# A transformer block on one core: one accumulator bank and four banks for maxima in attention, a written order and other splitting in the first projections, and the value bias added at the normalisation

## The chip, the core and the metric

The kernel runs on one core of a Trainium2 chip. A core has five engines that work side by side, each with its own queue of instructions in order: TensorE (PE, matrix products; its weight loads are listed apart as PEld), VectorE (DVE), ScalarE (ACT), GpSimd (POOL) and SyncE (SP, which here only issues DMAs). Matrix products end in PSUM, which has eight banks of 128 partitions by 512 numbers of 32 bits. POOL does not touch PSUM in this kernel; ACT and DVE empty it. The metric is the time of one execution in microseconds (us); lower is better.

## The reference

A block with layer norms after each part: attention whose four projections each have a low-rank addition, then a mixture of experts. Input is `x` of 2 x 1024 tokens with 512 numbers.

```python
def lora_linear(x, W, b, Bm, Am):
    out = jnp.einsum('bld,od->blo', x, W) + b
    upd = jnp.einsum('blr,or->blo', jnp.einsum('bld,rd->blr', x, Bm), Am)
    return out + SCALING * upd                      # rank 16, SCALING 0.5
q, k, v = (_split(lora_linear(x, ...)) for q, k, v)  # 16 heads of 32
scores = jnp.einsum('bhqd,bhkd->bhqk', q, k) * SCALE
attn = jax.nn.softmax(scores, axis=-1)
out = jnp.einsum('bhqk,bhkd->bhqd', attn, v)
x = _layernorm(x + lora_linear(out, Wo, bo, Bo, Ao))
x = _layernorm(x + _moe(x, ...))   # 8 experts, capacity 256, hidden 704, and one shared expert
```

The rows of `attn` add up to one, so a bias that is added to every value vector comes out of attention as the same bias, added to the output of the head.

## The kernel before

Products of full accuracy are made from three products of numbers cut to a shorter format: a number is split into a high part (a cast by ACT) and a low part (number minus high part, by DVE or POOL), and high x high, low x high and high x low are added up in PSUM.

The work comes in three stages.

*First projections* (0 to about 158 us of the span). The low-rank factors are folded into the weights: `split_lora` splits the two factors, `fold_w` multiplies them, `split_w` adds the product to the weight and splits it. `load_lora`, `load_w` and `load_xk` issue the DMAs from SP. The first block of x is projected to q with the loop over the contraction outermost (`proj_all`), so that it can begin when a quarter of the weights is there. `store_qk` adds the bias, splits the result and sends it to DRAM; `proj_v` adds the value bias `bv_bc` (the bias spread over all partitions by a DMA) and sends v to DRAM. In the last of the four x blocks, the first 12 steps of maxima (below) are mixed in.

*Attention* (about 158 to 604 us). There are 16 units `u` (2 batches x 4 groups of 4 heads x 2 blocks of 512 queries), each of 8 steps `t` of 128 keys. A step has four heads `h`. The softmax needs each query's maximum first: `s1_step` makes a tile of scores with queries on the partitions (L203) and DVE reduces it (L211); 32 such tiles a unit run 12 steps ahead (`LEAD`). `finish_max` transposes the maxima (`mp`) and puts them into the query operand as two more rows, so that the second score product (`st_step`, L641) comes out with the maximum subtracted, keys on the partitions. ACT turns it into exponentials `pt` (L650). Every second step `av_step` multiplies the exponentials of the two steps before by v into the unit's accumulator `avs[u]` in PSUM (L660). For the row sums, `adds` adds the exponentials of a unit's steps up: by DMAs that accumulate ("dd", issued by POOL, L678), by POOL ("pp", L681), or in the last units by DVE ("vv", L681). `finish` sums over the partitions on PE (`sm`, L694), `invert` takes the reciprocal by way of DRAM, and `normalize` makes the output in three parts: 0, accumulator times reciprocal (L733); 1, its high part `at_h` (ACT L738, DVE L736 in two units); 2, its low part `at_l` (L740). `oproj` projects a batch's output, adds the residual (`load_res`, `add_res`) and takes the norm's statistics.

The order of all engines in attention is written out. In each step there are four slots, one behind each head's score product. `S_AT[k][q]` gives for step k of a unit and slot q how many maxima tiles come before and after the other work of that slot. `FIN`, `REC` and `NRM` place `finish`, `invert` and the parts of `normalize`, as (units later, step, slot); `ADDS` places the additions, `RES_AT` and `RES_ADDS` the residuals. The key `None` holds for all units that are not named.

PSUM in the first two stages: three banks `one` (second scores, maxima transposes, row sums, projections), two banks `avp` (accumulators), three banks `s1p` (maxima tiles). `ptp` holds `PTB` buffers of exponentials in SBUF.

*Experts* (from about 604 us): the shared expert, the routing, and eight experts; the last expert's rows are normalised by `norm_root` (POOL) and `norm_rows_act` (ACT) and stored by POOL's indirect DMAs.

`tc.manual_schedule(engines=...)` keeps the named engines in the order of the program; the others are ordered by the framework's planner. In the first stage PE is always in program order (`MAN1`), and ACT, DVE and POOL (`MAN0`) only up to the end of the first `split_k` loop.

Of the kernel before, what the change touches and what calls it, by code (L numbers as in the profile page):

```python
# [9 lines left out]
F32 = mybir.dt.float32  # L10
# [22 lines left out]
LEAD = 12  # L33
LATE, OP_ONE = (0,), 1
NS = NU * 8
WARM, WCOL = 4, 256
OPER = 4
PTB = 14
OHB = 3
# [18 lines left out]
FIN = {None: (1, 4, 1), NU - 3: (1, 3, 1), NU - 2: (1, 2, 3)}  # L58
REC = {None: (1, 6, 3), NU - 3: (1, 5, 3)}
NRM = {  # L60
    None: ((2, 1, 0), (2, 1, 2), (2, 1, 2)),
    NU - 3: ((2, 0, 1), (2, 0, 1), (2, 0, 1)),
    NU - 2: ((1, 4, 1), (1, 4, 1), (1, 4, 1)),
# [3 lines left out]
S_AT = (  # L67
# [4 lines left out]
)  # L72
# [40 lines left out]
def kernel(  # L113
    ctx, tc, xT, x, wT, bqk, bvo, lora, wg, w13, w2, s13, s2, out
):
# [19 lines left out]
    pool.memset(expo, -0.5)  # L135
    bqk_sb = const.tile([P, 8], F32, name="bqk_sb")
    bo_bc = const.tile([P, D], F32, name="bo_bc")
# [96 lines left out]
    with ExitStack() as ph1, tc.manual_schedule(engines=MAN1):  # L234
# [15 lines left out]
        wl = [wp.tile([P, KC, D], F32R, name=f"wl{i}") for i in range(3)] + [wo_l]  # L250
        bv_bc = wp.tile([P, D], F32, name="bv_bc")

        def load_lora(i):
            raws = []
            for j in range(2):
                raws.append(next(lraw_s)[0:LR])
                sp.dma_start(out=raws[j], in_=lora[i, j])
            return raws
# [12 lines left out]
        def prep_w(i, raws, ba=None):  # L271
            ba = ba or split_lora(i, raws)
            for k, lp in enumerate([fold_w(i, ba, k) for k in range(KC)]):
                split_w(i, k, raws, lp)

        def split_lora(i, raws):
            ba = []
            for j, lo in ((0, 64), (1, 32)):
                t_ = sg.tile([LR, D], F32R, name=f"lora{i}{j}", tag=f"lora{j}", bufs=1)
                act.copy(t_, raws[j])  # L280
                rows = slice(lo, lo + R)
                dve.tensor_tensor(t_[rows], raws[j][rows], f(t_[rows]), ALU.subtract)
                ba.append(t_)
            return ba

        def fold_w(i, ba, k):
            if k == KC - 1:
                lp = avp.tile([P, 512], F32, name=f"lp{i}{k}", tag="av")
            else:
                lp = s1p.tile([P, 512], F32, name=f"lp{i}{k}", tag="s1")  # L290
            pe.matmul(lp, ba[0][:, k * P : k * P + P], ba[1], start=True, stop=True)
            return lp
# [47 lines left out]
        def store_qk(tb, w, g, o):  # L340
            b, c0 = tb // 2, (tb % 2) * 512
            bias = bqk_sb[:, w * 4 + g : w * 4 + g + 1]
            oh = sg.tile([P, 512], F32R, name=f"oh{tb}{w}{g}", tag="oh", bufs=OHB)
            ol = sg.tile([P, 512], F32R, name=f"ol{tb}{w}{g}", tag="ol", bufs=OHB)
            act.activation(oh, o, AF.Identity, bias=bias)  # L345
            dve.scalar_tensor_tensor(ol, o, bias, f(oh), ALU.add, ALU.subtract)
            sp.dma_start(out=qk_d[w, b, g, 0][:, c0 : c0 + 512], in_=f(oh))
            sp.dma_start(out=qk_d[w, b, g, 1][:, c0 : c0 + 512], in_=f(ol))

        def proj_v(tb, xs, t4):  # L350
            o = bank1(f"v{tb}{t4}")
            n = 0
            for k in range(KC):
                hi, lo = (z[:, t4 * P : t4 * P + P] for z in xs[k])
                for lhs, rhs in ((hi, wh[2]), (lo, wh[2]), (hi, wl[2])):
                    pe.matmul(o, lhs, rhs[:, k, :], start=n == 0, stop=n == 11)
                    n += 1
                    if n % 6 == 0:
# [29 lines left out]
        for k in range(KC):  # L388
            load_wk(1, k, r1)
        sp.dma_start(out=bqk_sb, in_=bqk)  # L390

        with tc.manual_schedule(engines=MAN0):
            dve.memset(bo_bc, 0.0)
            warm("hot", WARM)
            ba = split_lora(0, r0)
            lps = [fold_w(0, ba, k) for k in range(KC)]
            warm("warm", 1)
            os_ = [bank1(f"o00{g}") for g in range(NG)]
            xs = []

            def split_k(k):
                split_w(0, k, r0, lps[k])
                xs.append(split_xk(0, k, x0[k]))


            def proj_all(k):
                hi, lo = xs[k]
                for i, (w_, x_) in enumerate(((wh, hi), (wl, hi), (wh, lo))):
                    for g in range(NG):
                        a = w_[0][:, k, g * P : g * P + P]  # L410
                        pe.matmul(os_[g], a, x_, start=k + i == 0, stop=False)

            pool.memset(f(Ks[0][96:98, :, :]), -1.0)
            for k in range(KC):
                split_k(k)
                if k == 1:
                    ba1 = split_lora(1, r1)
            pool.memset(f(Ks[1][96:98, :, :]), -1.0)
        for k in range(KC):
# [5 lines left out]
            if k == KC - 3:  # L425
                prep_w(1, r1, ba1)
        for tb in range(4):
            if tb == 0:
                for g in range(NG):
                    store_qk(0, 0, g, os_[g])  # L430
                    if g == 1:
                        sp.dma_start(out=bv_bc, in_=bvo[0:1, :].partition_broadcast(P))
                        r2 = load_w(2)
                for g in range(NG):
                    proj_qk(tb, xs, 1, g)
                    if g == 1:
                        prep_w(2, r2)
            else:
# [7 lines left out]
            for t4 in range(4):  # L446
                proj_v(tb, xs, t4)
                if t4 == 1 and tb < 3:
                    xn = split_x(tb + 1, xr)
            if tb == 0:  # L450
                sp.dma_start(out=bo_bc, in_=bvo[1:2, :].partition_broadcast(P))
                prep_w(3, load_w(3))
# [169 lines left out]
    with ph2, tc.manual_schedule(engines={mybir.EngineType.PE}):  # L622
# [31 lines left out]
        def av_step(t):  # L654
# [4 lines left out]
            for h in range(4):  # L659
# [7 lines left out]
                )  # L667

        def adds(t):
            u, kc = t // 8, t % 8  # L670
# [57 lines left out]
        def normalize(u, parts=(0, 1, 2)):  # L728
            g, qb = u // 2, u % 2
            cs = slice(qb * 512, qb * 512 + 512)  # L730
            hi, lo = at_h[:, g % NG, cs], at_l[:, g % NG, cs]
            if 0 in parts:
                dve.tensor_tensor(avs[u], avs[u], fin[u], ALU.mult)  # L733
            if 1 in parts:
                if u in NRM_DVE:
                    dve.tensor_copy(hi, avs[u])  # L736
                else:
                    act.copy(hi, avs[u])  # L738
            if 2 in parts:
                dve.tensor_tensor(lo, avs[u], f(hi), ALU.subtract)  # L740

# [59 lines left out]
        for t in range(NS):  # L801
# [433 lines left out]
    with tc.manual_schedule(engines=MAN4):  # L1235
# [123 lines left out]
```

## Time and profile before

| | |
|---|---|
| time, three runs | 1046.94, 1047.83, 1050.71 us (median 1047.83) |
| profiled execution, its own time | 1045.05 us |
| its span, first to last instruction | 1043.3 us |
| mean granted TensorE clock | 0.991 |
| first projections | 0 to 158 us |
| attention | 158 to 604 us |
| experts, to the end | 604 to 1043 us |

A row of groups gives line, engine, operation, output and inputs by the program's names, shapes and count, then busy time in us, mean duration of one in ns, and the idle time of the engine in front of it with what ended it. A row of the timeline gives start, duration, engine, line, operation, names and shapes, how many in a row, and in brackets the idle time before. A matmul's end is modelled and overlaps the next one's start, so that a PE that is busy all the time can still be held up; the distance of starts tells.

### The profile page before, as it was taken

What the parts mean: (1) busy time and instruction counts of PE and PEld (TensorE: products, weight loads), DVE (VectorE), ACT (ScalarE), POOL (GpSimd) and SP (SyncE); (2) the same over time, 40 slices, a digit from 0 to 9 for tenths busy, and PEclk for the clock granted to TensorE, in tenths of its full rate; (3) what the DMA queues carried; (4) which work ended last, traced back from release to release, by engine and by line L of the source; (5) the groups of instructions that cost most, each with busy time, mean ns of one, the idle gap of its engine ahead of it and who ended that gap; (6) DMA issues with size and microseconds to landing.
All of it is one profiled execution on the core that took longest, in us unless ns stands there. A gap on an engine that the chain in (4) does not pass through costs nothing. (4 is left out here: it accounts for less than half of the span.)

```text
span 1043.3 us, 15652 instructions
## 1 busy us (share of the span) xinstructions
PE 1016.6 (97%) x5606; PEld 722.7 (69%) x5606; DVE 676.1 (65%) x1156; ACT 520.4 (50%) x985; POOL 536.1 (51%) x404
## 2 busy tenths in 40 slices
PE   8999999999999999999999799999999999999994
PEld 6888784544444456654444279988788899999994
DVE  7732788788878877788877774222253467777752
ACT  5422206666666656576666645222132356555662
POOL 4000006889888977879895155000006056666674
PEclk9999999999999999999999899999999999999998
DMA  9876875686868783587974532000109667777721
GB/s 291 283 230 210 248 211 118 125 186 137 190 134 187 160 181 83 115 168 155 197 163 92 132 104 70 22 21 1 40 1 293 212 198 237 255 244 258 224 82 60
DMA packets 87374, 164.75 MB, mean 158 GB/s; under 512 B 15944, under 2 KB 24648, under 8 KB 87296
## 3 DMA queue, kind: packets, MB, share of 16 engines
q1 hardware_dynamic: 74240, 117.59, 38.8%
q0 software_dynamic: 13056, 46.16, 19.9%
q8 instruction: 44, 0.72, 0.3%
q14 instruction: 34, 0.28, 0.1%
HBM read 96.10 MB, written 33.80 MB: 125 GB/s over the span
## 5 line engine op out<-in xcount | busy, mean ns | idle before, releaser
L211 DVE TENSOR_REDUCE mt<-s 128x1 f32<-128x512 f32 x512 | 318.4, 681 | 75.2 <-PE s L203 75.1
L650 ACT ACTIVATE pt<-st 128x512 f32<-128x512 f32 x512 | 266.3, 618 | 147.5 <-PE st L641 145.6
L681 POOL TENSOR_TENSOR pt<-pt,pt 128x1024 f32<-128x1024 f32 x112 | 264.2, 2387 | 33.4 <-DMA pt<-pt 18.1
L203 PE MATMUL s<-ks,qs 96*128 96x512 f32 x512 | 196.1, 416 | 1.5 <-DVE mt L211 1.0
L641 PE MATMUL st<-qs,ks 98*128 98x512 f32 x512 | 189.3, 417 | 2.7 <-ACT pt L650 1.7
L678 POOL DMA_DIRECT2D pt<-pt x64 | 56.3, 1008 | 195.2 <-PE s L203 164.7
L641 PEld LDWEIGHTS st<-qs,ks 98*128 98x128 f32 x512 | 94.8, 189 | 72.5 <-ACT pt L650 26.8
L203 PEld LDWEIGHTS s<-ks,qs 96*128 96x128 f32 x512 | 94.2, 188 | 72.7 <-DVE mt L211 44.5
L924 PE MATMUL h<-xthe,w13s 128*128 128x256 f32 x704 | 129.9, 283 | 0.0
L924 PEld LDWEIGHTS h<-xthe,w13s 128*128 128x128 f32 x704 | 110.6, 191 | 0.4
L924 PE MATMUL h<-xtle,w13s 128*128 128x256 f32 x352 | 100.2, 285 | 0.0
L912 POOL TENSOR_TENSOR w2s<-w2r,w2s 128x512 fp32r<-128x512 f32 x42 | 65.8, 1588 | 64.9 <-ACT w2s L911 56.3
L1114 POOL DMA_INDIRECT xd_d<-x1a,slot_i x8 | 7.9, 985 | 139.3 <-DVE slot_i L1111 137.2
L660 PE MATMUL av<-pt,vt 128*32 128x512 f32 x512 | 64.0, 613 | 4.3 <-DVE at_l L740 4.3
L924 PEld LDWEIGHTS h<-xtle,w13s 128*128 128x128 f32 x352 | 67.3, 191 | 0.7
L660 PE MATMUL av<-pt,x1b 128*32 128x512 f32 x512 | 61.6, 598 | 0.0
L1010 PE MATMUL y<-w2s,hs 128*128 128x512 f32 x260 | 60.9, 390 | 0.0
L1010 PEld LDWEIGHTS y<-w2s,hs 128*128 128x128 f32 x260 | 48.3, 188 | 10.2 <-DVE hs L992 0.5
L589 DVE TENSOR_TENSOR w13s<-x1a,w13s 128x1024 fp32r<-128x1024 f32 x32 | 47.0, 1468 | 6.5 <-ACT w13s L583 6.5
L345 ACT ACTIVATE oh<-o,bqk_sb 128x512 fp32r<-128x512 f32 x32 | 21.9, 689 | 57.7 <-PE o L330 52.8
L583 ACT CAST w13s<-x1a 128x1024 fp32r<-128x1024 f32 x32 | 33.4, 1044 | 25.6 <-DMA x1a<-in_w_dram 19.4
L330 PE MATMUL o<-xh,wh 128*128 128x512 f32 x116 | 45.3, 391 | 0.0
(567 smaller groups left out, 1699.4 us busy)
## 6 DMA issues: line engine op xcount, KB each, us to landing
pt<-pt POOLq DMA_DIRECT2D x64, 512.0 KB, 7.9
x1a<-in_w_dram SPq DMA_DIRECT2D x32, 512.0 KB, 6.5
w2r<-in_w_dram SPq DMA_DIRECT2D x42, 256.0 KB, 3.2
ks<-qkd SPq DMA_DIRECT2D x36, 256.0 KB, 3.9
qkd<-oh SPq DMA_DIRECT2D x32, 256.0 KB, 2.9
qkd<-ol SPq DMA_DIRECT2D x32, 256.0 KB, 2.5
qs<-qkd SPq DMA_DIRECT2D x30, 256.0 KB, 5.1
qs<-qkd SPq DMA_DIRECT2D x36, 128.0 KB, 6.2
```

The lines of the kernel that those rows point to most:

```text
L203: pe.matmul(s1, Qs[u % 3][0:96, h, qt * P : qt * P + P], Ks[g % 2][0:96, h, kh * 512 : kh * 512 + 512], start=True, stop=True,)
L211: dve.tensor_reduce(mts[u][:, c, kh : kh + 1], s1, AX.X, ALU.max)
L330: pe.matmul(o, lhs, rhs, start=k + i == 0, stop=k + i == KC + 1)
L589: (pool if e < 0 else dve).tensor_tensor(lo, raw, f(hi), ALU.subtract)
L641: pe.matmul(sb, Ks[g % 2][:, h, kc * P : kc * P + P], Qs[u % 3][:, h, :], start=True, stop=True,)
L650: act.activation(pts[t, h // 2][:, h % 2, :], sb, AF.Exp, scale=SCALE)
L660: pe.matmul(avs[u][32 * h : 32 * h + 32, :], vts[g][:, kc, 32 * h : 32 * h + 32], pts[t, h // 2][:, h % 2, :], start=kc == 0, stop=kc == 7 ...
L678: pool.dma_start(out=pts[to, pr], in_=pts[i, pr], accum_op=ALU.add)
L681: eng.tensor_tensor(accs[u, pr], accs[u, pr], pts[i, pr], ALU.add)
L912: pool.tensor_tensor(hl[:, 1, :], raw, f(hl[:, 0, :]), ALU.subtract)
L924: pe.matmul(hp[:, j * 256 : j * 256 + 256], lhs, rhs[:, k, :], start=n == 0, stop=n == 11,)
L1010: pe.matmul(o, lhs, rhs, start=n == 0, stop=n == 16)
```

## The change

- PSUM: one bank `avp` and four `s1p`. A unit's accumulator is copied to SBUF by ACT (`av_out`, two buffers `ae`) at the first step of the next unit, and `normalize` reads that copy; the last unit is still read in PSUM. `PTB` is 13. The first output projection of batch 1 and all folded weights take `s1p` banks.
- `S_AT` has other places for the 32 maxima tiles of a unit. Near the end of attention, `REC`, `NRM`, `ADDS` and `RES_ADDS` have other places.
- The value bias is not added in `proj_v`, which becomes an ACT copy, but per partition in parts 1 and 2 of `normalize`. The three biases come in one small tile; `bv_bc` and its DMA go.
- First projections: the second low-rank factor is loaded and split first, the other one in the first weight in two pieces; x is split ahead of the weight; k's low-rank factors are split one step later; the low parts of k's weights are made by POOL; ACT, DVE and POOL are in program order up to the end of the first block of x; v's weights are loaded ahead of the first stores.
- The last half of the last expert's rows is scaled by DVE, not by ACT.

```diff
-LATE, OP_ONE = (0,), 1
+LATE, OP_ONE = (0,), 0
-PTB = 14
+PTB = 13
-REC = {None: (1, 6, 3), NU - 3: (1, 5, 3)}
+REC = {None: (1, 6, 3), NU - 3: (1, 5, 1)}
 NRM = {
     None: ((2, 1, 0), (2, 1, 2), (2, 1, 2)),
-    NU - 3: ((2, 0, 1), (2, 0, 1), (2, 0, 1)),
+    NU - 3: ((1, 7, 3), (1, 7, 3), (1, 7, 3)),
 S_AT = (
-    ((0, 0), (0, 1), (1, 0), (1, 0)), ((0, 0), (0, 1), (1, 1), (0, 0)),
-    ((0, 2), (1, 0), (0, 0), (0, 2)), ((0, 0), (0, 1), (0, 2), (0, 0)),
-    ((0, 1), (1, 2), (0, 1), (1, 1)), ((1, 0), (0, 0), (2, 0), (1, 0)),
-    ((0, 0), (1, 0), (0, 1), (1, 0)), ((0, 1), (1, 0), (0, 0), (2, 0)),
+    ((2, 0), (0, 0), (1, 0), (0, 0)), ((0, 0), (2, 0), (1, 0), (0, 1)),
+    ((0, 0), (1, 1), (0, 1), (0, 0)), ((0, 0), (1, 1), (0, 1), (0, 1)),
+    ((0, 1), (1, 1), (1, 1), (2, 0)), ((0, 0), (0, 2), (1, 0), (0, 1)),
+    ((0, 1), (1, 0), (1, 0), (0, 0)), ((0, 1), (0, 1), (0, 1), (0, 1)),
-    NU - 2: {1: "bb1 dd01", 3: "dd23 vv4", 4: "vv5", 5: "vv6 vv3", 6: "vv7"},
+    NU - 2: {1: "bb1 dd01", 3: "dd23 vv4", 4: "vv5", 5: "vv6", 6: "vv3 vv7"},
-RES_ADDS = tuple(t + 3 for t in RES_AT[:14]) + (119, 120)
+RES_ADDS = tuple(t + 3 for t in RES_AT[:14]) + (114, 115)
...
-    avp = one_ps.enter_context(tc.tile_pool(name="avp", bufs=2, space=PSUM))
-    s1p = one_ps.enter_context(tc.tile_pool(name="s1p", bufs=3, space=PSUM))
+    avp = one_ps.enter_context(tc.tile_pool(name="avp", bufs=1, space=PSUM))
+    s1p = one_ps.enter_context(tc.tile_pool(name="s1p", bufs=4, space=PSUM))
...
         def prep_w(i, raws, ba=None):
             ba = ba or split_lora(i, raws)
-            for k, lp in enumerate([fold_w(i, ba, k) for k in range(KC)]):
-                split_w(i, k, raws, lp)
+            lps = [fold_w(i, ba, k) for k in range(KC)]
+            split_high(i, 0, raws, lps[0])
+            for k in range(KC):
+                if k < KC - 1:
+                    split_high(i, k + 1, raws, lps[k + 1])
+                split_low(i, k, raws)
...
+            cut = P if i == 0 else D
+            for j, lo, cs in ((1, 32, (0, D)), (0, 64, (0, cut)), (0, 64, (cut, D))):
+                if cs[0] < cs[1]:
+                    cs = slice(*cs)
+                    act.copy(ba[j][:, cs], raws[j][:, cs])
+                    rows = slice(lo, lo + R)
+                    dve.tensor_tensor(
+                        ba[j][rows, cs], raws[j][rows, cs], f(ba[j][rows, cs]), ALU.subtract
+                    )
...
-            dve.tensor_tensor(wl[i][:, k, :], raw, f(wh[i][:, k, :]), ALU.subtract)
+            (pool if i == 1 else dve).tensor_tensor(
+                wl[i][:, k, :], raw, f(wh[i][:, k, :]), ALU.subtract
+            )
...
-            dve.tensor_tensor(vv, o, bv_bc, ALU.add)
+            act.copy(vv, o)
...
             def split_k(k):
+                xs.append(split_xk(0, k, x0[k]))
                 split_w(0, k, r0, lps[k])
-                xs.append(split_xk(0, k, x0[k]))
...
-                if k == 1:
+                if k == 2:
                     ba1 = split_lora(1, r1)
-            pool.memset(f(Ks[1][96:98, :, :]), -1.0)
...
             if k == KC - 3:
-                prep_w(1, r1, ba1)
+                with tc.manual_schedule(engines=MAN0):
+                    prep_w(1, r1, ba1)
+                    pool.memset(f(Ks[1][96:98, :, :]), -1.0)
+        r2 = load_w(2)
         for tb in range(4):
+            block = ExitStack()
+            if tb == 0:
+                block.enter_context(tc.manual_schedule(engines=MAN0))
...
+        def av_out(u):
+            raws[u] = ap.tile([P, 512], F32, name=f"ae{u}", tag="ae", bufs=2)
+            act.copy(raws[u], avs[u])
...
+            av = raws.get(u, avs[u])
             if 0 in parts:
-                dve.tensor_tensor(avs[u], avs[u], fin[u], ALU.mult)
+                dve.tensor_tensor(av, av, fin[u], ALU.mult)
+
+            b_ = bias_sb[:, 8 + g % NG : 9 + g % NG]
             if 1 in parts:
                 if u in NRM_DVE:
-                    dve.tensor_copy(hi, avs[u])
+                    dve.tensor_scalar(hi, av, b_, None, ALU.add)
                 else:
-                    act.copy(hi, avs[u])
+                    act.activation(hi, av, AF.Identity, bias=b_)
             if 2 in parts:
-                dve.tensor_tensor(lo, avs[u], f(hi), ALU.subtract)
+                dve.scalar_tensor_tensor(lo, av, b_, f(hi), ALU.add, ALU.subtract)
...
                 between[AVQ].append(lambda: (av_step(t - 2), av_step(t - 1)))
+                if k == 0:
+                    between[AVQ].append(lambda: av_out(u - 1))
...
-            norm_root(outs[j])
-            norm_rows_act(bases[j], bases[j], outs[j])
+            norm_root(outs[j], hf == 0)
+            if hf == 0:
+                norm_rows_act(bases[j], bases[j], outs[j])
+            else:
+                mv, sc = outs[j]
+                dve.tensor_scalar(
+                    bases[j], bases[j], mv[:, 0:1], sc[:, 1:2], ALU.subtract, ALU.mult
+                )
```

More of the change, by code (lines that the diff above doesn't have):

```diff
@@ L113 @@
 def kernel(
-    ctx, tc, xT, x, wT, bqk, bvo, lora, wg, w13, w2, s13, s2, out
+    ctx, tc, xT, x, wT, bias, bo, lora, wg, w13, w2, s13, s2, out
 ):
@@ L135 @@
     pool.memset(expo, -0.5)
-    bqk_sb = const.tile([P, 8], F32, name="bqk_sb")
+    bias_sb = const.tile([P, 12], F32, name="bias_sb")
     bo_bc = const.tile([P, D], F32, name="bo_bc")
@@ L250 @@
         wl = [wp.tile([P, KC, D], F32R, name=f"wl{i}") for i in range(3)] + [wo_l]
-        bv_bc = wp.tile([P, D], F32, name="bv_bc")
         def load_lora(i):
-            raws = []
-            for j in range(2):
-                raws.append(next(lraw_s)[0:LR])
+            raws = [next(lraw_s)[0:LR] for j in range(2)]
+            for j in (1, 0):
                 sp.dma_start(out=raws[j], in_=lora[i, j])
@@ L272, in prep_w @@
             ba = ba or split_lora(i, raws)
-            for k, lp in enumerate([fold_w(i, ba, k) for k in range(KC)]):
-                split_w(i, k, raws, lp)
-        def split_lora(i, raws):
[L277 to L283, printed above, removed]
+            lps = [fold_w(i, ba, k) for k in range(KC)]
[4 more added lines that the diff above has]
+                split_low(i, k, raws)
+        def split_lora(i, raws):
+            ba = [
+                sg.tile([LR, D], F32R, name=f"lora{i}{j}", tag=f"lora{j}", bufs=1)
+                for j in range(2)
+            ]
+            cut = P if i == 0 else D
[7 more added lines that the diff above has]
+                    )
             return ba
         def fold_w(i, ba, k):
[L287 to L290, printed above, removed]
+            lp = s1p.tile([P, 512], F32, name=f"lp{i}{k}", tag="s1")
             pe.matmul(lp, ba[0][:, k * P : k * P + P], ba[1], start=True, stop=True)
@@ L341, in store_qk @@
             b, c0 = tb // 2, (tb % 2) * 512
-            bias = bqk_sb[:, w * 4 + g : w * 4 + g + 1]
+            b_ = bias_sb[:, w * 4 + g : w * 4 + g + 1]
             oh = sg.tile([P, 512], F32R, name=f"oh{tb}{w}{g}", tag="oh", bufs=OHB)
             ol = sg.tile([P, 512], F32R, name=f"ol{tb}{w}{g}", tag="ol", bufs=OHB)
-            act.activation(oh, o, AF.Identity, bias=bias)
-            dve.scalar_tensor_tensor(ol, o, bias, f(oh), ALU.add, ALU.subtract)
+            act.activation(oh, o, AF.Identity, bias=b_)
+            dve.scalar_tensor_tensor(ol, o, b_, f(oh), ALU.add, ALU.subtract)
             sp.dma_start(out=qk_d[w, b, g, 0][:, c0 : c0 + 512], in_=f(oh))
@@ L389 @@
             load_wk(1, k, r1)
-        sp.dma_start(out=bqk_sb, in_=bqk)
+        sp.dma_start(out=bias_sb, in_=bias)
         with tc.manual_schedule(engines=MAN0):
@@ L430 @@
                     store_qk(0, 0, g, os_[g])
-                    if g == 1:
-                        sp.dma_start(out=bv_bc, in_=bvo[0:1, :].partition_broadcast(P))
-                        r2 = load_w(2)
+                ba2 = split_lora(2, r2)
                 for g in range(NG):
@@ L436 @@
                     if g == 1:
-                        prep_w(2, r2)
+                        prep_w(2, r2, ba2)
             else:
@@ L449 @@
                     xn = split_x(tb + 1, xr)
+            block.close()
             if tb == 0:
-                sp.dma_start(out=bo_bc, in_=bvo[1:2, :].partition_broadcast(P))
+                sp.dma_start(out=bo_bc, in_=bo.partition_broadcast(P))
                 prep_w(3, load_w(3))
@@ L667, in av_step @@
                 )
+        raws = {}
+        def av_out(u):
+            raws[u] = ap.tile([P, 512], F32, name=f"ae{u}", tag="ae", bufs=2)
+            act.copy(raws[u], avs[u])
         def adds(t):
@@ L1334 @@
         "wT": np.stack([a("W" + n).T.reshape(KC, P, D) for n in "qkvo"]),
-        "bqk": np.concatenate([a("b" + n).reshape(4, P).T for n in "qk"], axis=1),
-        "bvo": np.stack([a("bv"), a("bo")]),
+        "bias": np.concatenate([a("b" + n).reshape(4, P).T for n in "qkv"], axis=1),
+        "bo": a("bo").reshape(1, D),
         "lora": np.stack([rows3(a("B" + n), a("A" + n).T) for n in "qkvo"]),
```

## The prediction

> **What bounds the kernel now.** I read the page first, then the groups by line, then the waits, windows and timeline of attention (about 158 to 600 us of the span), because most of the diff lies there.
>
> ```profile
> PE 1016.6 (97%) x5606; PEld 722.7 (69%) x5606; DVE 676.1 (65%) x1156; ACT 520.4 (50%) x985; POOL 536.1 (51%) x404
> L211 DVE TENSOR_REDUCE mt<-s 128x1 f32<-128x512 f32 x512 | 318.4, 681 | 75.2 <-PE s L203 75.1
> L681 POOL TENSOR_TENSOR pt<-pt,pt 128x1024 f32<-128x1024 f32 x112 | 264.2, 2387 | 33.4 <-DMA pt<-pt 18.1 <-ACT pt L650 13.5 <-ACT mh L224 1.2
> ...
> 300.00:360.00 60.00, 60.00 (x336) 29.11 (x335) 47.95 (x85) 38.61 (x78) 52.31 (x30) 1.00 0.81 174
> ...
> PEld s L203 <- DVE mt L211: 43.3, 107, 0.8
> PEld st L641 <- ACT pt L650: 21.0, 96, 0.3
> ```
>
> Lines one to three are from the page and its groups. The window line has, after its length, busy time (and count) of PE, PEld, DVE, ACT, POOL: in 60 us of attention PE is never idle, POOL is busy 87%, DVE 80%, ACT 64%. The last two are the waits of 160 to 560 us: PE waits mostly for a PSUM bank that DVE must empty, less for one that ACT must. These waits of weight loads overstate: in the timeline, matmul starts that follow each other at 0.234 us when nothing holds them show 30.2 us of excess from 170 to 560 us, of which about 13.2 is in front of a maxima matmul (bank from DVE), 8.3 in front of a score matmul (bank from ACT), and the rest the change to and from accumulation. The period of a unit (mp transposes at 222.7, 249.2, 275.8) is 26.5 us.
>
> Next, what DVE and POOL do to each other. One unit, then two places where a DVE instruction with both inputs in SBUF meets POOL, then a third; last, the tail's PE.
>
> ```profile
> 313.75 9.40 POOL L681 TENSOR_TENSOR pt<-pt,pt 128x1024 f32<-128x1024 f32 x4
> 324.25 1.77 POOL L678 DMA_DIRECT2D pt<-pt  x2 [1.09 <-PE s L203]
> ...
> 316.95 0.69 DVE L733 TENSOR_TENSOR av<-av,rb 128x512 f32<-128x512 f32 x1
> 320.45 0.68 DVE L740 TENSOR_TENSOR at_l<-av,at_h 128x512 fp32r<-128x512 f32 x1
> ...
> 568.36 4.12 DVE L681 TENSOR_TENSOR pt<-pt,pt 128x1024 f32<-128x1024 f32 x1 [0.62 <-ACT pt L650]
> 568.38 3.01 POOL L749 TENSOR_TENSOR x1b<-x1b,bo_bc 128x512 f32<-128x512 f32 x2
> ...
> 852.49 3.47 DVE L589 TENSOR_TENSOR w13s<-x1b,w13s 128x1024 fp32r<-128x1024 f32 x1
> 852.32 2.55 POOL L912 TENSOR_TENSOR w2s<-w2r,w2s 128x512 fp32r<-128x512 f32 x2
> ...
> 877.00 1.69 DVE L589 TENSOR_TENSOR w13s<-x1b,w13s 128x1024 fp32r<-128x1024 f32 x1
> 876.31 4.79 POOL L912 TENSOR_TENSOR w2s<-w2r,w2s 128x512 fp32r<-128x512 f32 x3
> ...
> 577.82 0.50 PE L641 MATMUL st<-qs,ks 98*128 98x512 f32 x1 [0.24 <-ACT pt L650]
> 582.64 3.64 PE L660 MATMUL av<-pt,vt 128*32 128x512 f32 x16 [4.32 <-DVE at_l L740]
> 586.06 1.93 PE L694 MATMUL sm<-pt,ones 128*32 128x512 f32 x8
> ```
>
> The reader is to see that today's normalisation (L733, L740) runs in the middle of POOL's run of adds and is not touched by it: 0.69 and 0.68 us, since its accumulator is in PSUM and only one input in SBUF. A DVE add of two SBUF tensors, 1.21 us alone, took 4.12 us at 568.36 and 3.47 us at 852.49: each ended 1.1 us after the second of two POOL adds. It did not get in between them. At 877.00 it did (1.69 us); there POOL's next add still waited for an ACT cast (877.06 to 877.6).
>
> **The change, part by part.**
>
> *Normalisation from SBUF (the largest term).* L733 and L740 now read the copied accumulator in SBUF with a second SBUF operand. The Trainium skill, "SBUF — State Buffer", section "Who interferes with whom", says that such a DVE instruction and a POOL instruction that reads SBUF share a read port as an exclusive lock for the whole instruction, the later one blocking entirely. It speaks against this change, and the rows agree on the blocking. The rule as worded gives a wait for the instruction in progress; the rows at 568.36 and 852.49 show two. At 13 units' multiplication before 560 us, POOL's add in progress had 13.9 us left in all; at 11 of them more adds are queued behind it without a gap. For these 11, the add in progress has 1.2 us left on average, with the next one 3.5 us (plus 2.36), to the end of the run 6.3 us. While DVE is held, PE can fill the four maxima banks: in the new S_AT the fifth maxima matmul after the multiplication has 10 matmuls in front, 2.3 us. It then needs the multiplication (0.69) and one reduction (0.60). Delay of PE per unit = wait + 1.3 - 2.3. By the rule's one instruction: 0.2 us, taken as nothing, and the later subtraction (L740's successor) is held once more, 1.2 us, mostly under the same banks: 0 to 0.5 us, 3 us in all. By the rows' two: 2.5 us, and the subtraction meets the last add, 0.8 more: 3.3 x 11 = 36 us. To the end of the run: 5.3 x 11 = 58 us. I take two, as both rows with a queued second add show. Queued behind the held instruction are all maxima reductions; PE waits for them, then ACT (exponentials) for PE, and POOL's next DMA adds for PE (324.25), so the delay is not made up.
>
> *Four maxima banks.* Of 13.2 us in front of maxima matmuls at most all goes; DVE at 80% leaves it room, but POOL is near: from DMA add to the end of its run 25.4 us (297.7 to 323.15) of 26.5. I take 6 us off (0 to 13). The new S_AT keeps 32 maxima a unit.
>
> *One accumulator bank, copied out.* 15 ACT copies of PSUM, 0.58 us by the L708 row: 8.7 us. ACT idles 120 us there waiting for PE; without that cover, all 8.7. A late exponential can hold a score bank, so plus 1 us (0 to 3). The next accumulation comes two steps (6 us) later, so the single bank is free. L738's cast becomes an ACTIVATE with bias, 0.61 to between 0.69 (L345) and 0.81 (L618): hidden likewise. The subtraction becomes a SCALAR_TENSOR_TENSOR, 0.75 (L346) for 0.68: in DVE's slack. PTB 13: the thirteenth buffer is needed when step 4 begins, and the next are freed by the row-sum matmuls in front of its third score; no wait expected, and without that order some 2 us a unit.
>
> *Tail.* Unit 15's accumulation waited at 577.8 for unit 13's normalisation (4.32 us), and ran at half speed after the idle time (3.64 for 1.85 us; clock 0.83 in 580 to 600). With the copy that wait goes. The row sums of unit 14 then need DVE's adds, ending at 580.5, or 577.6 if POOL's two residual adds (moved from steps 119, 120 to 114, 115) no longer hold the add at 568.36. PE from 577.9: 1.85 and 0.95 give 580.7 to 581.6 instead of 587.9: minus 6.3 to 7.2. The rest is a chain DVE, PE, ACT that shifts along. I take 6.7; below, 2 if the next wait (ACT's exponentials) catches it.
>
> *First projections.* First real matmul at 8.09 us, behind two lora casts and subtractions, then 0.69 fold, 0.62 weight cast, 0.61 x cast. With the second lora factor first, the other cut at 128 columns (its 0.80 us subtraction shrinks) and x before the weight, it loses most of the x cast and some 0.5 us: minus 1.0 (0 to 1.2, as the clock rises only at 11.2). PE has no gap over 0.35 us from there to 110 us, and the new order keeps its operands ahead: w1's four low parts move to POOL (1.19 each by L316, for 0.69), done near 22 us, needed by 23. If they are late, up to 2 us. SP: the value-bias broadcast goes (0.33); load_w(2) is put in front of the stores, but its six issues already stood at 12.3 to 17.0, before the first store at 20.8. POOL's 3.5 us memset moves behind the low parts; unit 2 is the first to need it. 16 value additions go from DVE (0.69) to ACT copies (0.59); the first score matmul's wait for one at 156.4 (1.2 us) goes: minus 1.2.
>
> *End.* The last row scaling moves from POOL 0.26 and ACT 0.81 to one DVE instruction, at most L736's 0.69, at least half of it: minus 0.5 (0.4 to 0.7).
>
> *Sum.* 36 - 6 + 1 - 6.7 - 1.0 - 1.2 - 0.5 = 21.6. The profiled execution took 1045.05 us (span 1043.3 and 1.75 around it), 2.8 below the median of the runs, 1047.83. 1045.05 + 21.6 = 1066.7, on the median's scale 1069.5: 1070.
>
> **The rivals.**
> 1. *DVE gets the port after one instruction* (877.00 speaks for it, and the rule as worded): 3 for blocking, the banks' gain 8: 3 - 8 + 1 - 9.4 = -13.4, 1034. It ends on the faster side; it decides where POOL lets a waiting DVE in between queued adds. Against it: both places with a queued second add. Chance 0.27.
> 2. *DVE waits for the whole run of adds*: 58 - 6 + 1 - 9.4 = +43.6, 1091. For it: no run longer than two is shown to let DVE in. Against: DVE's delay also shifts the phases, and a bank stall lets POOL finish earlier against PE.
> 3. *Break-even*: a wait between, about 2.4 us (PE 1.4 a unit, 15 in all), is paid back by tail, start and banks: 1048. This is the point from which the sign turns.
> 4. *The fourth bank does nothing*, as POOL's 25.4 us binds: the forecast plus 6.
>
> **How the numbers follow.** DVE held for two adds or more: 0.68, split into 0.40 for the forecast (1055 to 1080; 0.10 of it with rival 4) and 0.28 for rival 2 (1080 to 1095). Rival 3, within 0.5% (5.2 us, about what a measurement of this kernel can tell from no change): 0.05. Faster: 0.27, rival 1. The forecast's own range is 1055 to 1080; the range that leaves out 2 in 10 runs from 1032 to 1089.
>
> **What would show it.** Right: L733 and the new subtraction well above 0.7 us, ending with a POOL add; a unit's period of 29 to 31 us instead of 26.5; PE waiting for DVE mt in stretches of over 1 us after each multiplication; DVE busy (held) share up, POOL's share down. In the tail no 4.3 us wait in front of L660. Wrong: L733 at 0.7 to 2 us and a period under 26.5. Start: first L411 near 7.1 us. End: no ACT row scaling of the last half.

## The result, and the profile after

The changed kernel takes 1108.14 us (median of six runs, 1104.08 to 1111.92), the kernel before 1048.08 us in the runs beside it: 5.67% more (ratio 1.0567, 95% interval 1.0534 to 1.0601). The profiled execution took 1104.08 us (span 1102.4). The forecast was 1070, with a range up to 1089. The sign was right, and so was the cause of the largest term: DVE is held by POOL. How long it is held was wrong, and the clock behind each wait was left out; rival 2 is nearer.

Where the time went, from the starts of marked matmuls in both traces:

| stretch (us) | before | after | difference |
|---|---|---|---|
| start to the last v projection's last matmul | 155.19 | 156.39 | +1.2 |
| to the maxima transposes of unit 1 | 14.7 | 13.7 | -1.0 |
| to the maxima transposes of unit 15 | 394.7 | 459.4 | +64.7 |
| to the last output projections | 39.2 | 32.2 | -7.0 |
| to the first matmul of the shared expert | 25.3 | 25.3 | 0 |
| to the end of the span | 414.3 | 415.4 | +1.1 |

So nearly the whole loss lies in the middle of attention. (The 1.1 us of the experts stay unexplained.) First the page: busy times and, further down, the share of each of the 40 slices.

```profile
PE 1031.7 (94%) x5606; PEld 739.5 (67%) x5606; DVE 722.2 (66%) x1138; ACT 539.5 (49%) x1016; POOL 541.3 (49%) x407
...
PE   8999999899888889998998899999999999999995
...
PEclk9999999998888899999988999999999999999998
...
L211 DVE TENSOR_REDUCE mt<-s 128x1 f32<-128x512 f32 x512 | 317.8, 680 | 77.2 <-PE s L203 77.0
L700 POOL TENSOR_TENSOR pt<-pt,pt 128x1024 f32<-128x1024 f32 x112 | 263.5, 2379 | 25.9 <-DMA pt<-pt 19.8
L203 PE MATMUL s<-ks,qs 96*128 96x512 f32 x512 | 195.8, 421 | 44.3 <-DVE mt L211 44.1
L753 DVE TENSOR_TENSOR ae<-ae,rb 128x512 f32<-128x512 f32 x14 | 69.6, 4972 | 10.3 <-DMA rb<-rd 10.3
```

The multiplication of the normalisation (L753, before: L733) takes 4972 ns on average; before it took 694. PE, never idle in the window of before, now stands 44.1 us in front of maxima matmuls (L203). POOL's additions and DVE's reductions are unchanged, 2379 and 680 ns: POOL is not slowed, DVE alone is held. PE falls to 8 in nine slices of attention, and in five of them PEclk does too.

The window of 60 us (after its length: busy time and count of PE, PEld, DVE, ACT, POOL, then the clock), and the waits from 160 to 620 us:

```profile
300.00:360.00 60.00, 51.29 (x263) 26.20 (x262) 49.55 (x68) 34.26 (x68) 42.20 (x25) 0.89 0.58 125
```

```profile
PEld s L203 <- DVE mt L211: 61.1, 36, 5.8
ACT at_h L760 <- DVE ae L753: 47.7, 11, 5.4
PE s L203 <- DVE mt L211: 44.1, 10, 5.5
PEld st L653 <- ACT pt L662: 21.6, 33, 4.6
```

In the same 60 us PE issues 263 matmuls instead of 336, at a clock of 0.89 instead of 1.00. The waits for DVE grew from 43.3 to 61.1 us but from 107 to 36 in number: fewer and long. The ACT line is one that the prediction left out: the cast L760 waits for the multiplication, 11 times, and the exponentials behind it in ACT's order wait with it.

One unit in the timelines of DVE, POOL and PE:

```profile
309.54 5.32 DVE L753 TENSOR_TENSOR ae<-ae,rb 128x512 f32<-128x512 f32 x1 [1.74 <-DMA rb<-rd]
314.78 1.87 DVE L211 TENSOR_REDUCE mt<-s 128x1 f32<-128x512 f32 x3
316.57 0.73 DVE L762 SCALAR_TENSOR_TENSOR at_l<-ae,bias_sb,at_h 128x512 fp32r<-128x512 f32 x1
```

```profile
303.70 9.39 POOL L700 TENSOR_TENSOR pt<-pt,pt 128x1024 f32<-128x1024 f32 x4
313.05 1.26 POOL L771 TENSOR_TENSOR x1a<-x1a,bo_bc 128x512 f32<-128x512 f32 x1
```

```profile
310.25 0.80 PE L653 MATMUL st<-qs,ks 98*128 98x512 f32 x2
315.51 1.39 PE L203 MATMUL s<-ks,qs 96*128 96x512 f32 x2 [4.46 <-DVE mt L211]
...
318.11 3.64 PE L672 MATMUL av<-pt,x1b 128*32 128x512 f32 x16
```

The multiplication starts in POOL's third addition, sits through the fourth and through the residual addition L771, and ends 0.55 us after that (313.05 + 1.26 = 314.31; 309.54 + 5.32 = 314.86). Eleven units show this, with 4.5 to 6.94 us (mean 6.04); each ends 0.55 us after the last instruction of POOL's unbroken run. (Two units whose multiplication falls among output projections show 0.76 and 1.72.) PE stands still for 4.46 us until DVE reduces again. Then the 16 matmuls of L672 take 3.64 us, twice their 1.92 elsewhere. The clock in five stretches around it:

```profile
309.00:312.00 3.00, 2.05 (x9) 1.18 (x7) 2.46 (x1) 1.50 (x4) 3.00 (x2) 1.00 0.80 223
312.00:317.00 5.00, 1.49 (x3) 1.08 (x4) 5.00 (x5) 2.11 (x4) 2.30 (x2) 0.78 0.09 26
317.00:321.00 4.00, 4.00 (x19) 0.96 (x18) 2.70 (x5) 1.26 (x3) 0.00 (x0) 0.50 0.00 0
321.00:325.00 4.00, 4.00 (x20) 2.35 (x20) 2.31 (x4) 2.72 (x6) 2.70 (x4) 0.92 0.34 66
325.00:330.00 5.00, 5.00 (x40) 1.94 (x32) 4.47 (x10) 2.24 (x5) 3.41 (x3) 1.00 1.06 197
```

Behind the wait the granted clock is 0.50 for a whole stretch of 4 us, with PE busy all the time. A unit's period (from one unit's maxima transposes to the next one's), 26.5 us before, is 26.1 and 25.4 where no normalisation lies in it, and 31.9 to 33.7 in ten others. In the three that hold output projections it is 36.0, 37.5 and 33.1, before 29.8, 37.0 and 33.7.

The tail went as forecast. Its PE timeline:

```profile
638.33 0.49 PE L653 MATMUL st<-qs,ks 98*128 98x512 f32 x1 [0.31 <-ACT pt L662]
638.75 1.92 PE L672 MATMUL av<-pt,vt 128*32 128x512 f32 x16
640.61 1.88 PE L653 MATMUL st<-qs,ks 98*128 98x512 f32 x7
```

No accumulation of unit 15 stands behind a normalisation any more (4.32 us before), and none runs at half speed.

### The profile page after: what moved, and what is told of

Same layout as the page of the kernel before. It is cut to its first block, busy times and chain, and to the rows that moved or that the text cites. A ratio compares the mean times of both kernels' runs of the same rounds, so it can differ in the third digit from the quotient of the medians.

```text
span 1102.4 us, 15691 instructions
## 1 busy us (share of the span) xinstructions
PE 1031.7 (94%) x5606; PEld 739.5 (67%) x5606; DVE 722.2 (66%) x1138; ACT 539.5 (49%) x1016; POOL 541.3 (49%) x407
## 5 line engine op out<-in xcount | busy, mean ns | idle before, releaser
L700 POOL TENSOR_TENSOR pt<-pt,pt 128x1024 f32<-128x1024 f32 x112 | 263.5, 2379 | 25.9 <-DMA pt<-pt 19.8
L203 PE MATMUL s<-ks,qs 96*128 96x512 f32 x512 | 195.8, 421 | 44.3 <-DVE mt L211 44.1
L653 PE MATMUL st<-qs,ks 98*128 98x512 f32 x512 | 201.2, 423 | 7.1 <-ACT pt L662 6.9
L203 PEld LDWEIGHTS s<-ks,qs 96*128 96x128 f32 x512 | 100.5, 196 | 85.4 <-DVE mt L211 61.1
L753 DVE TENSOR_TENSOR ae<-ae,rb 128x512 f32<-128x512 f32 x14 | 69.6, 4972 | 10.3 <-DMA rb<-rd 10.3
L672 PE MATMUL av<-pt,x1b 128*32 128x512 f32 x512 | 69.5, 665 | 0.0
L672 PE MATMUL av<-pt,vt 128*32 128x512 f32 x512 | 66.9, 637 | 0.0
L353 ACT ACTIVATE oh<-o,bias_sb 128x512 fp32r<-128x512 f32 x32 | 21.7, 688 | 55.3 <-PE o L338 51.9
L338 PE MATMUL o<-xl,wh 128*128 128x512 f32 x116 | 45.4, 392 | 0.0
```

The costliest lines, as they stand in the source:

```text
L203: pe.matmul(s1, Qs[u % 3][0:96, h, qt * P : qt * P + P], Ks[g % 2][0:96, h, kh * 512 : kh * 512 + 512], start=True, stop=True,)
L653: pe.matmul(sb, Ks[g % 2][:, h, kc * P : kc * P + P], Qs[u % 3][:, h, :], start=True, stop=True,)
L672: pe.matmul(avs[u][32 * h : 32 * h + 32, :], vts[g][:, kc, 32 * h : 32 * h + 32], pts[t, h // 2][:, h % 2, :], start=kc == 0, stop=kc == 7 ...
L700: eng.tensor_tensor(accs[u, pr], accs[u, pr], pts[i, pr], ALU.add)
L753: dve.tensor_tensor(av, av, fin[u], ALU.mult)
```

## The experiments

Theory: the loss is DVE held through POOL's whole run of SBUF reads, once a unit, plus the clock that falls behind each PE wait. Rivals: the single bank and ACT's copies; the first projections; a wait of one addition that something else multiplies. The kernel before took 1044.0 to 1046.4 us in the runs beside these.

**The normalisation later.** One edit to the changed kernel; units 6 and 7 stay, since the output projection needs them.

```diff
-    None: ((2, 1, 0), (2, 1, 2), (2, 1, 2)),
+    None: ((2, 3, 0), (2, 3, 0), (2, 3, 1)),
+    6: ((2, 1, 0), (2, 1, 2), (2, 1, 2)),
+    7: ((2, 1, 0), (2, 1, 2), (2, 1, 2)),
```

> The changed kernel with the three parts of normalisation placed ten slots later for the ordinary units (step 3 of the second unit after, where POOL has only DMAs to issue), units 6 and 7 left where they are. Nothing else changes. Theory A (port: DVE's multiplication of two SBUF tensors waits for POOL's whole run of adds, and PE loses its clock behind it): the multiplication falls back to 0.7 us (under 2 us in nearly all units), the unit's period from 33 to 25.5-26.5 us, the time to 1030-1045 us. Theory B (the new places of the maxima, the ACT copies or the single accumulator bank slow attention, and the long multiplication is only where it shows): the period stays over 30 us and the time over 1090 us.

Measured: 1051.11 us, ratio 1.0079 (1.0052 to 1.0106). Most of the loss, about 51 us of 60, went with this one table entry, so the single bank, the copies and the start can hold only what is left. The upper end of the expectation was missed by 6 us: the multiplication still took 1.2 to 4.2 us in nine units, since POOL's run now reached into step 3; each of the nine again ends 0.55 us after POOL's last addition.

```profile
L755 DVE TENSOR_TENSOR ae<-ae,rb 128x512 f32<-128x512 f32 x14 | 29.8, 2130 | 0.0
```

**Two SBUF inputs alone.** The kernel before, with one more DVE multiplication behind L733 in 13 units whose product is not used. PTB is 13 to make room.

```diff
+                if u < NU - 3:
+                    dum = ap.tile([P, 512], F32, name=f"dum{u}", tag="dum", bufs=1)
+                    dve.tensor_tensor(dum, fin[u], fin[u], ALU.mult)
```

> The kernel before, with one more DVE instruction behind each multiplication of units 0 to 12: the reciprocal tile in SBUF times itself into a spare tile (two SBUF inputs), and 13 buffers of exponentials for 14. The product is not used. Banks, maxima and everything else as before. Theory A: this instruction alone does what the change did: it lasts 5 to 7 us in most units, the period goes from 26.5 to over 32 us (one bank less for PE to run ahead), and the time to 1105-1135 us. Theory B: the instruction costs its 0.7 us beside other work, 1048-1058 us.

**One SBUF input.** The same with `dve.tensor_tensor(dum, avs[u], fin[u], ALU.mult)`, the first input in PSUM.

> The same as the kernel with the spare product, but the extra instruction multiplies the accumulator in PSUM with the reciprocal (one SBUF input). The product is not used. Theory A: 0.7 us each, untouched by POOL; the period stays at 26.5 to 27, the time within 1046-1057 us. If any further DVE instruction at this place, or 13 buffers, were the cost: as slow as with two SBUF inputs.

Measured: 1124.33 us (one run) with two, 1047.15 us with one (ratio 1.0038, 1.0023 to 1.0054). The extra instruction in the one and in the other:

```profile
L736 DVE TENSOR_TENSOR dum<-rb 128x512 f32<-128x512 f32 x13 | 67.4, 5184 | 0.0
```

```profile
L736 DVE TENSOR_TENSOR dum<-av,rb 128x512 f32<-128x512 f32 x13 | 9.0, 692 | 0.4
```

Same place, same operation, same size: 5184 against 692 ns. What decides is the second SBUF input. The ordinary units have periods of 33.3 to 34.5 us in the first run, so this instruction by itself is enough for a loss as large as the changed kernel's.

**The clock.** The changed kernel, with 16 matmuls in step 2, whose product is not used; first in units 2 to 13, then only in units 2 to 7 and 11 to 13.

```diff
+        def fill(t):
+            hot = one.tile([P, 512], F32, name=f"fill{t}", tag="one")
+            for i in range(16):
+                pe.matmul(hot, wo_h[:, 0, 0:P], wo_h[:, 1, :], start=True, stop=True)
...
+            if k == 2 and 2 <= u < NU - 2:
+                between[0].append(lambda: fill(t))
```

> The changed kernel with 16 idle products of 512 columns on PE (about 3.7 us, results unused) in step 2 of units 2 to 13, just ahead of the maxima product that waits behind the multiplication. They add PE work that fits in the wait. Theory C (a part of the 33 us is that the clock falls to half for some 6 us behind each wait of 4.5 us): the granted clock stays near 1.0 through attention, the period falls from 33 to 30-31 us, the time to 1070-1085 us although work was added. Without the clock's part: 1108 or more.

> The changed kernel with 16 filler matmuls (their product is not used) in step 2 as in the earlier run, but only in units 2 to 7 and 11 to 13, where no output projection already fills PE's wait. Theory (a part of the loss is the granted clock, which falls to half for about 6 us behind each wait of 4 to 6 us): the filler, which is 3.7 us of PE's own work and lies in the wait, keeps the clock at 1.0; periods 31.0 instead of 31.9 to 33.5 in at least seven of the nine units and unchanged elsewhere, 10 to 16 us less than the changed kernel in all, ratio to the kernel before 1.041 to 1.047. Rival (the clock is of no account, the period is set by DVE's wait alone): no shorter than the changed kernel, ratio 1.055 or more.

Measured: 1099.21 us (one run) and 1099.16 us (ratio 1.0486, 1.0449 to 1.0523), both short of what was expected. In the first the units of the output projections grew to 41.0 and 36.4 us, since there the filler adds work. The second leaves those alone; its periods are 30.9 to 31.1 in five of the nine units and 32.1 to 33.9 in four, where seven were expected. (The profiled execution of the second was its slowest, 1106.34 us; the periods are read from it.) The same stretches as above, in the second:

```profile
312.00:317.00 5.00, 3.32 (x15) 2.43 (x14) 5.00 (x4) 1.68 (x3) 2.74 (x2) 1.00 0.30 70
317.00:321.00 4.00, 4.00 (x26) 1.94 (x25) 3.13 (x6) 2.07 (x5) 0.35 (x1) 1.00 0.00 0
```

More work on PE made the kernel faster: 1.0486 against 1.0567, some 8 us (give or take 5, by the two intervals), because PE that works through the wait keeps its clock (26 matmuls instead of 19 in the four microseconds behind it). The nine units of the second run say the same: the five of 30.9 to 31.1 us have no stretch at a granted clock of 0.50, three of the other four (32.8 to 33.9) kept one of 3.41 us. In the fourth, 32.1, the clock stayed full. The clock is a part of the loss of at least some 8 us.

**Out of POOL's run.** The first edit with step 4 in place of step 3.

```diff
-    None: ((2, 1, 0), (2, 1, 2), (2, 1, 2)),
+    None: ((2, 4, 0), (2, 4, 0), (2, 4, 1)),
```

> The changed kernel with the normalisation of all units but 6 and 7 at step 4 of the second unit after (parts 0 and 1 in slot 0 or behind, part 2 in slot 1), not step 1: after POOL's run of additions (0.4 to 20.5 us after a unit's maxima transposes in the run with step 3, up to 23 with a residual addition) and before the next (27.8). Theory (the loss is DVE held through POOL's run): the multiplication takes 0.7 to 1.3 us in all the moved units, the periods of 26 to 30 us with step 3 all become 26, some 14 us less than with step 3, ratio to the kernel before 0.990 to 0.998; and the period of 26.0 against 26.5 before is what the fourth maxima bank and the new places of the maxima are worth, 6 us. Rival (POOL and DVE share the port all the time, wherever it is put, or ACT's copies hold the unit up): multiplications still at 2 us or more, periods of 28 and more, ratio 1.005 or higher.

Measured: 1047.79 us, ratio 1.0038 (1.0023 to 1.0053).

```profile
L764 DVE SCALAR_TENSOR_TENSOR at_l<-ae,bias_sb,at_h 128x512 fp32r<-128x512 f32 x15 | 15.5, 1035 | 2.7 <-ACT at_h L762 2.6
L755 DVE TENSOR_TENSOR ae<-ae,rb 128x512 f32<-128x512 f32 x14 | 15.4, 1098 | 0.8 <-DMA rb<-rd 0.8
```

In the mean of 1098 ns lies unit 6, unmoved, with 6.43 us; the other multiplications take 0.68 to 0.77. The ratio is above the 0.998 expected. Two things stand out: the period with unit 6's wait is 37.5 us against 29.8 before, and in the second batch the period is 27.1 to 27.3 against 26.5 to 26.9, where the subtraction L764 was held twice (2.9 us). From unit 1 to unit 7 it gains 2.5 us on before (157.1 against 159.6), 0.4 a unit. This is what fourth bank, new places and single bank gave together in the first batch; the second gives 1.6 back (81.6 against 80.0 from unit 11 to 14). Together they gained about 1 us in these two stretches, not 6; the fourth bank alone was not run.

**A POOL instruction that reads nothing.** The changed kernel, with `pool.memset(expo, -0.5)` (one column) behind each of POOL's additions.

> The changed kernel, with one POOL memset of a one-column tile (no SBUF input) behind each of POOL's additions. Theory A (POOL keeps the port from one reading instruction to the next as long as they follow back to back, and an instruction that reads nothing lets DVE in): the multiplication waits for one addition at most, 1 to 3.5 us instead of 4.5 to 6.9, periods 27 to 30, time 1050 to 1075. Theory B (POOL has the port until its queue holds nothing that could run, whatever the kind): the multiplication still takes 4.5 to 7 us, periods of 33, time 1104 or a few us more for the memsets.

**A gap between the additions.** The same with a small DMA, issued by POOL.

```diff
+                        if op[pr] == "p":
+                            n = next(gaps) % 16
+                            pool.dma_start(out=gap[0:1, n : n + 1], in_=expo[0:1, :])
```

> The changed kernel with one small DMA (4 bytes from one SBUF tile to another) issued by POOL behind each of its additions, where the memset did not let DVE in. Theory (DVE gets the port when POOL executes no instruction of its own for a while, as the issue of a DMA, 0.8 to 1.2 us each in this trace, leaves it): the multiplication waits for one addition at most, 1 to 3.5 us; POOL's longer work (8 issues a unit) makes the time hard to forecast, 1060 to 1110. Rival (only an empty or waiting POOL queue lets DVE in): 5 to 8 us as before, and 1105 or more.

Measured: 1108.69 and 1132.06 us (one run each). The memset let nothing in: ten multiplications of 5.65 to 8.16 us and one of 4.56, at the end of the run. The DMA issue leaves 0.45 us between two additions, and this happens (POOL, then DVE):

```profile
284.52 2.39 POOL L702 TENSOR_TENSOR pt<-pt,pt 128x1024 f32<-128x1024 f32 x1
286.84 0.50 POOL L705 DMA_DIRECT2D gap<-expo  x1
287.36 2.38 POOL L702 TENSOR_TENSOR pt<-pt,pt 128x1024 f32<-128x1024 f32 x1
289.67 0.53 POOL L705 DMA_DIRECT2D gap<-expo  x1
290.21 2.35 POOL L702 TENSOR_TENSOR pt<-pt,pt 128x1024 f32<-128x1024 f32 x1
292.49 0.50 POOL L705 DMA_DIRECT2D gap<-expo  x1
293.01 2.38 POOL L702 TENSOR_TENSOR pt<-pt,pt 128x1024 f32<-128x1024 f32 x1
```

```profile
285.94 7.21 DVE L758 TENSOR_TENSOR ae<-ae,rb 128x512 f32<-128x512 f32 x1 [0.20 <-issue]
```

The multiplication passes two gaps and ends 0.6 us after the third addition, at 293.15, while a fourth follows. Of 13 such waits DVE got in at the second gap in three, at the third in eight, at the fourth in two, and never at the first. So both theories of this run fall short: a gap of 0.45 us does let DVE in, but not each one. What makes POOL yield stays open.

**The tail alone.** The kernel before, with the copies of units 13 and 14 only, the changed `REC`, `NRM`, `ADDS`, `RES_ADDS`, PTB 13, and the last half scaled by DVE.

```diff
+                if k == 0 and u - 1 >= NU - 3:
+                    between[AVQ].append(lambda: av_out(u - 1))
...
-    NU - 3: ((2, 0, 1), (2, 0, 1), (2, 0, 1)),
+    NU - 3: ((1, 7, 3), (1, 7, 3), (1, 7, 3)),
```

> The kernel before, with three parts of the change alone: the accumulators of units 13 and 14 copied out by ACT and their normalisation, the residual additions and DVE's additions at the end of attention placed as in the changed kernel; PTB 13; the last half of rows scaled by DVE. Theory (these parts are worth what the comparison of the traces shows, 7.0 us in the tail and 0.6 at the end, and need neither the one accumulator bank nor the fourth for maxima): ratio 0.992 to 0.994, from the maxima transposes of unit 15 to the first output projection 32 us instead of 39. Rival (the tail is only shorter there because the delays before it left other engines ahead): ratio 0.998 or higher, the stretch 36 us or more.

Measured: 1038.22 us, ratio 0.9944 (0.9931 to 0.9957): faster than both kernels, and just short of the 0.992 to 0.994 expected. Unit 15's transposes to the last output projections take 33.8 us instead of 39.2, and the accumulation that waited 4.32 us follows at once:

```profile
578.45 0.50 PE L641 MATMUL st<-qs,ks 98*128 98x512 f32 x1 [0.25 <-ACT pt L650]
578.88 1.92 PE L660 MATMUL av<-pt,vt 128*32 128x512 f32 x16
580.62 1.04 PE L700 MATMUL sm<-pt,ones 128*32 128x512 f32 x8
```

The tail's gain needs neither the single bank nor the fourth one.

**The rest.** The changed kernel with the attention of before: its banks, tables and PTB, the normalisation from PSUM.

> The changed kernel with the attention of the kernel before (two accumulator banks and three for maxima, its places of maxima and of the last units' work, 14 buffers of exponentials, the normalisation read from PSUM at once). What is left of the change: the first projections, the value bias at the normalisation, the last half scaled by DVE. The prediction's sum says -1.0 -1.2 -0.5 = -2.7 us, ratio 0.997. The comparison of the traces says that the start gave nothing (+1.2 at the first score product) and the end 0.6: ratio 1.000 to 1.002. If the start cost 3 us or more by something that the traces hide, 1.003 or higher.

**The split of k's factors put back.**

```diff
-                if k == 2:
+                if k == 1:
                     ba1 = split_lora(1, r1)
```

> The run with the attention of the kernel before and the changed first projections, with one thing put back: k's low-rank factors are split behind the second quarter of the weights, as before, not behind the third. Theory (what made the changed start slower is that the folds of k's weights, in PE's program order, wait for that split: 2.74 us of PE at 16.67, and 1.2 to 1.6 us more in front of the last q matmuls): both waits go, the first score product comes at 155 to 156 us instead of 158.5, ratio to the kernel before 0.998 to 1.000. Rival (the written order of ACT and DVE or POOL's low parts are what holds PE, whatever the split's place): still over 157.5, ratio 1.001 to 1.003.

Measured: 1045.85 us, ratio 1.0016 (1.0009 to 1.0023), and with the split put back 1044.92 us, ratio 1.0000 (0.9991 to 1.0010). The folds of k's weights in the first, then in the second:

```profile
16.67 1.23 PE L300 MATMUL lp<-lora,lora 80*128 80x512 f32 x4 [2.74 <-DVE lora L290]
```

```profile
13.33 0.86 PE L300 MATMUL lp<-lora,lora 80*128 80x512 f32 x3
14.78 0.50 PE L300 MATMUL lp<-lora,lora 80*128 80x512 f32 x1 [0.59 <-DVE x1b L309]
```

The later split makes PE wait 2.74 us at the folds (1.25 in the changed kernel's own trace), which PE's order puts in the middle of q. Part of it is the same hold again: the second subtraction L290 took 1.47 us, ending 0.54 us after a POOL subtraction (L327). With the split put back, the first second-score product starts at 154.65 us instead of 158.46 (155 to 156 was expected; the kernel before has 155.89). So the start is no loss, and no gain that the times show.

**The parts that pay together.** That start and that tail in one kernel.

> The changed start with k's split put back, as in the run beside it, the value bias at the normalisation, and the end of attention and the last half as in the run of these parts alone (ratio 0.9944): the parts of the change that pay, without the single accumulator bank. If the parts add up: ratio 0.991 to 0.994, 1035 to 1038 us. If the start's part is worth nothing or the tail loses its gain to it: 0.994 to 0.997.

Measured: 1038.14 us, ratio 0.9937 (0.9924 to 0.9949). The interval overlaps with the tail alone; the start adds nothing that can be told.

## Why the prediction was right or wrong

*Normalisation from SBUF: the step that failed.* "I take two" was wrong: in all eleven units DVE waited for the whole run. The mean multiplication of 6.04 us is a wait of 5.35 (it takes 0.69 unheld). By the prediction's own formula (wait + 1.3 - 2.3) that is 4.35 us of PE a unit, 48 us in 11 units instead of 36. The traces agree. From unit 1 to unit 15, before and after (length, then busy time of PE, PEld, DVE, ACT, POOL):

```profile
169.91:564.59 394.68, 392.89 (x2126) 201.97 (x2127) 313.01 (x547) 255.79 (x499) 333.32 (x196) 1.00 0.71 152
170.09:629.53 459.44, 409.65 (x2126) 217.76 (x2126) 372.48 (x547) 265.86 (x512) 336.54 (x198) 0.93 0.63 131
```

PE's idle time, length less busy time, grows from 1.8 to 49.8 us: 48 us. Both rows that it rested on had runs of two additions, where "two" and "all" are the same; rival 2 said so and got 0.28. The second hold that it counted, on the subtraction, didn't occur in the changed kernel: it comes after the run, at 0.73 to 0.75 us.

The page that the prediction weighed, the Trainium skill, "SBUF — State Buffer", section "Who interferes with whom", speaks of a lock for a whole instruction. The part about two SBUF inputs is what the runs show (5184 against 692 ns). As a bound on the wait, one instruction, it would have given rival 1's 1034 us; the measurement decides.

*The clock: a term that was missing.* The other 16.8 us of the 64.7 are PE's busy time for the same 2126 matmuls, 409.65 us instead of 392.89. Behind each of the eleven waits (3.2 to 5.5 us) the granted clock is 0.50, for 6.83 us in nine units and 3.41 in two; behind the wait shown above:

```profile
314.85:321.68 6.83, 6.17 (x21) 2.04 (x22) 4.85 (x9) 3.37 (x6) 0.00 (x0) 0.50 0.00 0
```

PE is busy in 54 of these 68 us, so the lower clock can have cost at most 27 us; the filler shows at least some 8. How much of the 16.8 is the clock's alone is not separated further. The period is therefore 31.9 to 33.7 us, not the 29 to 31 forecast. Before's trace showed it: the prediction itself read 3.64 for 1.85 us behind the 4.32 us wait of the tail, and credited its end there, but did not charge it for each new wait of that length.

The Trainium skill, "TensorE: Matmul & The Clock Gate", section "HAM oscillation — how this bites in real kernels", has a rule that would have: no idle time of PE over about 3.4 us, or the matmuls that come next start at half the clock; and its part 1 has a window of about that length as what brings the clock back. Behind nine of the eleven waits the low clock lasted twice that. As a threshold the runs don't bear the rule out: in the run with step 3 PE waited 1.67 us in front of the matmul at 246.22, and this followed:

```profile
247.87:251.28 3.41, 3.41 (x18) 1.02 (x11) 1.50 (x4) 0.84 (x2) 2.68 (x2) 0.50 1.04 192
```

Other waits of that length, as the 1.68 us at 316.58 in the second filler run, left the clock at 1.00.

*The fourth bank*: -6 in the sum; about -1 together with the single bank in the run with step 4. *ACT's copies*: +1; nothing found against it. But the cast behind the multiplication stood 47.7 us and the exponentials with it. PE waits for DVE at the same time, so what this adds is not separated.

*Tail*: -6.7 in the sum, -7.0 in the traces, -5.4 alone. *End*: -0.5 against -0.6 (last expert's last matmul to the last store's: 5.58 to 4.96). *Value bias*: -1.2 against -1.0 in the stretch to unit 1.

*First projections*: -1.0 against +1.2. The change list had the later split of k's factors, and the prediction said that the order "keeps its operands ahead" without following the folds, which need that split and waited for it. The first real matmul, forecast at 7.1, came at 8.29 us here, and at 7.27 to 7.84 in the nine experiments with this start. ACT's timeline has x's DMA as what sets it, with the weight's cast in order behind the x cast:

```profile
7.10 0.62 ACT L323 CAST xh<-x1a 128x512 fp32r<-128x512 f32 x1 [2.41 <-DMA x1a<-in_xT_dram]
7.62 0.61 ACT L307 CAST wh<-x1b 128x512 fp32r<-128x512 f32 x1
```

*The rivals.* Rival 1 (one instruction) fell, and so did break-even. Rival 2 had 1091, and with 17 us for the clock 1108. That it would have met the time is in part luck: it had 58 us for the 48 of the wait, and its 6 us for the bank, of which little came, made up for half of that. Rival 4 was right in that the bank brought little, but whether POOL is the reason was not tested.

## What to carry to other kernels

Before a DVE operand moves from PSUM to SBUF, count how long POOL's longest unbroken run of work is, not how long one instruction is, and either keep one operand in PSUM or place the instruction where POOL waits. A wait of PE can cost more than its length, as the clock can fall behind it: look in the windows for the clock behind waits of the size that you are about to add. And where a change is a bundle, take the parts apart: here a few lines at the end of attention were worth 0.6%, and one place in a table cost 5%.

## What the runs showed of the hardware that was not expected

- A held DVE instruction of 512 columns ended 0.55 us after POOL's run. A POOL memset, which has no SBUF input, didn't end the hold, and a gap of 0.45 us ended it only sometimes (never the first of them, in 13 waits).
- Without any gap DVE did twice get in ahead of POOL's next instruction. In the run with step 4 a subtraction that started with the addition, at 488.25 us, took 2.91 us and the next addition 2.8 instead of 2.38. In the changed kernel the multiplication at 486.48 (1.72 us) ended 0.55 us after an addition, and the small L624 that followed it at once took 1.01 instead of 0.55 us. Why there and not elsewhere is open.
- 16 superfluous matmuls in each of nine units made the kernel some 8 us faster.
- A PE wait of 1.67 us was followed by 3.41 us at a granted clock of 0.50, in the run with step 3; others of that length were not.
